# Expert blocks of a routed feed-forward: rows loaded from a register address and turned by VectorE instead of TensorE

## The chip, the cores and the metric

The kernel runs as one program on one core of one Trainium2 chip. Its time is device microseconds of one execution; five executions took 2359.26 to 2365.59 us, with a median of 2361.71 us. Engines are named as the profile names them: PE (TensorE matmul), PEld (its weight loads), DVE (VectorE), ACT (ScalarE), POOL (GpSimd), SP (SyncE, which here only issues transfers). SPq is SP's queue of transfer instructions.

## The reference

Eight images of 256 channels on 32 x 32 points pass through two layers, all in float32. The first is multi-head attention (8 heads, 64 channels each) with a residual. The second works on tokens (1024 per image, 256 channels): a softmax attention with one weight matrix, and then a mixture of experts, which is the part that the change touches.

```python
def _moe(tokens, router_w, w1, b1, w2, b2):          # E = 8 experts, D = F = 256
    logits = tokens @ router_w.T
    probs = jax.nn.softmax(logits, axis=-1)
    rw, re = jax.lax.top_k(probs, 2)
    rw = rw / jnp.maximum(rw.sum(-1, keepdims=True), 1e-12)
    combine = jnp.zeros((N, E)).at[jnp.arange(N)[:, None], re].set(rw)
    out = tokens
    for e in range(E):
        h = jax.nn.gelu(tokens @ w1[e] + b1[e], approximate=False)
        out = out + combine[:, e:e+1] * (h @ w2[e] + b2[e])
    return out
```

Each token takes part in two of eight experts, and a sum over its two experts' outputs, weighted by its gates, is added to it.

## The kernel before

**Stages.** The images 0 to 6 go one after the other through layer 0 and the token attention. At the end of each, `dispatch` scatters every token's 256 values twice into a DRAM table `rows`, once into the region of each of its two experts (7168 rows per expert). When image 7 has passed layer 0, `experts` (lines 1017 to 1106) computes the outputs of all scattered rows of images 0 to 6 into a DRAM table `y`. After that image 7's token attention runs, then its own experts (`dense`), while `Results` gathers the rows of `y` and adds them to images 0 to 6.

**Blocks.** `plan` cuts the experts' regions into 63 blocks of BR = 256 rows, and computes for each block where its rows start (`row_at`) and where its expert's weights stand (`w_at`). Both are only known on the chip. A block has these steps:

- `fetch` (L1020 to L1047): an indirect transfer on POOL's queue (L1026) brings the packed weights `wb`, 128 rows of 5128 bytes (out of bounds, so nothing moves, where the buffer already has the expert); there are four buffers. A second one (L1035) brings the 256 rows, two per partition, into `xr` (three buffers). Four PE transposes (L1044) turn them into the PSUM tile `px`, and a DVE copy (L1046) takes it to `xb`, where the 256 channels lie on partitions.
- `hidden` (L1049): four float32 products `ph` (L1054), which the profile counts as eight, and two Gelu activations on ACT (L1064) into `hT`.
- `collect` (L1072): four products `pe` (L1079), again eight in the profile, a DVE addition of the bias (L1088) into `yb`, and a store of `yb` to `y` from SP (L1093).

The loop issues `hidden(b-1)`, `fetch(b)`, `collect(b-2)`. A scheduler lays out each engine's list of instructions from this, and `tc.issue_after` makes it put one instruction behind another. Every engine runs its own list strictly in order. On PE a block reads `ph` of one block, `px` of the next one and `pe` of the block before.

**Queues.** SP holds, beside the y stores, the loads of images, the quarter moves `aT` of the token attention (L697), the loads of the sums `o` (L1153), of the dense weights (L1233, L1237) and the stores of the output (L1226). A transfer issued from SP or ACT takes one of eight completion semaphores in turn, and waits until the transfer that had it eight transfers before is complete.

**Packed weights.** `pack` (L283) copies w1, w2, b1 and b2 once, early in the program, into the DRAM table `wpack`, such that a row of it is what one partition of `wb` needs.

**Bookkeeping on DVE.** `places` (L991) computes for each image and choice, from the plan, which row of `y` a token's output will be; it is issued as one piece after block 4's addition. Its results are `kept` for the gathers.

Of the kernel before, what the change touches and what calls it, by code (L numbers as in the profile page):

```python
# [10 lines left out]
F32 = mybir.dt.float32  # L11
# [8 lines left out]
def kernel(  # L20
# [39 lines left out]
    NWB = 3  # L60
    NXB = NWB + 1

    dram = ctx.enter_context(tc.tile_pool(name="dram", bufs=1, space=bass.MemoryType.DRAM))
# [72 lines left out]
    for e in range(E):  # L136
# [14 lines left out]
    )  # L151
    r_iota = const.tile([P, 1], F32, name="r_iota")
    nc.gpsimd.iota(
        r_iota, [[1, 1]], base=0, channel_multiplier=R, allow_small_or_imprecise_dtypes=True
    )
    ones = const.tile([P, P], F32, name="ones")
# [52 lines left out]
    NB = NT // NH2  # L209
    SQ = 32  # L210
    NQ = P // SQ

# [68 lines left out]
    def pack():  # L281


        wp = wpack.rearrange("(e p) c -> e p c", p=P)
        for dc in range(NCC):
            nc.sync.dma_start(  # L286
                wp[:, :, ts(dc, FF)], w1.rearrange("e (dc p) f -> dc e p f", p=P)[dc]
            )
        at = NCC * FF
# [147 lines left out]
    def layer0(b, xT, begun, routing, xs):  # L437
# [138 lines left out]
        for at in range(last + LAG + 1):  # L576
# [28 lines left out]
            elif at == last + 1:  # L605
                divide(last)
            if at == 0:
# [318 lines left out]
    def plan(group):  # L926
# [41 lines left out]
        base = tmp("p_base", [E])  # L968
        nc.vector.tensor_scalar(base, first, -float(BR), r_iota, ALU.mult, ALU.add)
        work = tmp("p_work", [nb, E])  # L970
# [3 lines left out]
        nc.vector.scalar_tensor_tensor(lo, b_iota[:, :nb], float(BR), lo, ALU.mult, ALU.add)  # L974
        nc.vector.tensor_scalar_min(lo, lo, float(cap - R))
        nc.vector.scalar_tensor_tensor(lo, e_of, float(cap), lo, ALU.mult, ALU.add)
# [16 lines left out]
    def places(group):  # L993

        first = group.first
        for b in group.items:
            gate, kept = group.kept[b]
            ats = []
            for k, (row, exp) in enumerate(kept):
# [15 lines left out]
                ats.append(at)  # L1015
            group.kept[b] = gate, ats

    def experts(group):
        n = group.n
        row_at, w_at = group.where  # L1020

        wbs_x = [*wbs, one.tile([P, WROW], F32, tag="v", name="wb_x")]

        def fetch(b):
            wb = wbs_x[b % NXB]
            nc.gpsimd.indirect_dma_start(  # L1026
                out=wb[:, :],
                out_offset=None,
                in_=wpack[:, :],
                in_offset=bass.IndirectOffsetOnAxis(ap=w_at[:, b : b + 1], axis=0),  # L1030
                bounds_check=E * P - 1,
                oob_is_err=False,
            )
            xr = rowp.tile([P, R, D], F32, tag="xr", name=f"xr_{n}_{b}")
            nc.gpsimd.indirect_dma_start(  # L1035
                out=xr.rearrange("p r d -> p (r d)"),
                out_offset=None,
                in_=group.rows[:, :],
                in_offset=bass.IndirectOffsetOnAxis(ap=row_at[:, b : b + 1], axis=0),
            )  # L1040
            px = big(f"px_{n}_{b}")
            for dc in range(NCC):
                for r in range(R):
                    nc.tensor.transpose(px[:, ts(dc * R + r, P)], xr[:, r, ts(dc, P)], ident)  # L1044
            xb = two.tile([P, NCC, BR], F32, tag="xb", name=f"xb_{n}_{b}")
            nc.vector.tensor_copy(xb.rearrange("p c t -> p (c t)"), px[:, : NCC * BR])  # L1046
            return xb  # L1047

        def hidden(b, xb):  # L1049
            wb = wbs_x[b % NXB]  # L1050
            ph = big(f"ph_{n}_{b}")
            for fc in range(NFC):
                for dc in range(NCC):
                    nc.tensor.matmul(  # L1054
                        ph[:, ts(fc, BR)],
# [7 lines left out]
            for fc in range(NFC):  # L1063
# [6 lines left out]
                )  # L1070
            return hT

        def collect(b, hT):
            wb = wbs_x[b % NXB]
            py = acc(f"pe_{n}_{b}")
            at = NCC * FF
            for r in range(R):
                for fc in range(NFC):
                    nc.tensor.matmul(  # L1079
                        py[:, ts(r, D)],  # L1080
                        hT[:, fc, ts(r, P)],
                        wb[:, at + fc * D : at + (fc + 1) * D],
                        start=(fc == 0),
                        stop=(fc == NFC - 1),
                    )
            at += NFC * D + NFC
            yb = two.tile([P, R, D], F32, tag="yb", name=f"yb_{n}_{b}")
            added = nc.vector.tensor_add(  # L1088
                yb,
                py.rearrange("p (r d) -> p r d", d=D),  # L1090
                wb[:, at : at + D].unsqueeze(1).to_broadcast([P, R, D]),
            )
            nc.sync.dma_start(group.y[ts(b, BR), :].rearrange("(p r) d -> p r d", r=R), yb)  # L1093
            if b == NXB:
                with tc.issue_after(added.ins):
                    places(group)


        rows, hiddens = {}, {}
        for b in range(group.nb + 2):  # L1100
            if b - 1 in rows:
                hiddens[b - 1] = hidden(b - 1, rows.pop(b - 1))
            if b < group.nb:
                rows[b] = fetch(b)
            if b - 2 in hiddens:
                collect(b - 2, hiddens.pop(b - 2))

# [237 lines left out]
    for b in range(B):  # L1345
# [6 lines left out]
        if b + 1 < B:  # L1352
# [5 lines left out]
            continue  # L1358
        experts(groups[0])
        others = Results(groups[0])  # L1360
# [56 lines left out]
```

## Time and profile before

| What | Value |
|---|---|
| Median of five executions | 2361.71 us |
| The profiled execution's own time | 2360.97 us |
| Its span | 2359.0 us |
| Mean granted clock of PE | 0.992 |
| PE busy / DVE busy / ACT busy / POOL busy over the span | 98% / 64% / 46% / 18% |
| First PE transpose of `xr` starts / last product `pe` ends | 1859.8 us / 2128.8 us |
| POOL transfers of rows (L1035) | 63, 956 ns each on POOL |
| DVE copies of `px` (L1046) | 63, 691 ns each |
| SP's y stores (L1093) | 63, 320 ns each on SPq |

Times in the tables of groups are busy times of a whole group and the mean of one instruction; matmuls are pipelined, so that the mean of one (381 ns for `ph`) is longer than the distance between two. The distance is read from the chain of work that ended last, which gives a whole run of products its share of the time. The time of DMA packets is given as a share of the 16 DMA engines' time.

### The profile page before, as it was taken

How to read it: one execution, taken by the hardware profiler on the slowest of the kernel's cores; microseconds unless marked ns; L12 is line 12 of the kernel's file. 1: busy time of each engine (PE TensorE's matmuls, PEld its weight loads, DVE VectorE, ACT ScalarE, POOL GpSimd, SP SyncE). 2: the span in 40 equal slices, each digit the busy share in tenths (PEclk: the TensorE clock that was granted, in tenths of full speed). 3: DMA queues.
4: the chain of work that ended last, by engine and by line, in shares of the span. 5: the costliest groups of instructions: out<-in, count | busy, mean ns of one | idle time of the engine just before them, and what ended most of it. 6: DMA issues, size and time to landing. Idle time of an engine off the chain costs nothing.

```text
span 2359.0 us, 37255 instructions
## 1 busy us (share of the span) xinstructions
PE 2305.4 (98%) x13375; PEld 1256.3 (53%) x13375; DVE 1513.0 (64%) x3660; ACT 1092.3 (46%) x1954; POOL 421.4 (18%) x391
## 2 busy tenths in 40 slices
PE   9999999999999999999999999999999999999798
PEld 3345534653456345633563356335643588885465
DVE  5775577567855785578557855786578653334755
ACT  3663366346634663466346634563556422223311
POOL 0000012000200020002000300030003144544563
PEclk9999999999999999999999999999999999999899
DMA  8995201020102010201030102010201266665664
GB/s 296 385 386 140 63 17 39 13 51 15 41 9 54 10 46 6 57 8 48 3 61 6 50 1 45 21 35 1 45 19 61 88 213 221 206 201 143 156 176 110
DMA packets 219232, 209.23 MB, mean 89 GB/s; under 512 B 120200, under 2 KB 162856, under 8 KB 217256
## 3 DMA queue, kind: packets, MB, share of 16 engines
q1 hardware_dynamic: 192952, 139.13, 19.7%
q0 software_dynamic: 25008, 67.20, 9.3%
q8 instruction: 107, 1.75, 0.3%
q10 hardware_dynamic: 1088, 0.52, 0.1%
q14 instruction: 77, 0.63, 0.1%
HBM read 108.88 MB, written 110.90 MB: 93 GB/s over the span
## 4 chain that ended last, share of the span: by engine, by line
PE 81%; SPq 8%; DVE 5%; DMA 2%; issue 1%; ACT 1%; another core or an unknown queue 1%; POOL 0%; DVEq 0%; ACTq 0%; POOLq 0%
PE po L541 17%; PE psc L464 16%; PE py L713 8%; PE ps L672 7%; PE pqk L346 6%; SPq L270 5%; PE ph L1054 4%; PE pe L1079 4%; PE pr L638 4%; PE pv L383 4%; PE px L657 2%; PE pdy L1307 2%; PE pdh L1283 2%; PE pqk L324 2%; SPq L286 1%
## 5 line engine op out<-in xcount | busy, mean ns | idle before, releaser
L505 ACT ACTIVATE ex<-psc,nmax 128x1024 f32<-128x1024 f32 x512 | 570.5, 1115 | 304.2 <-DVE scrap L488 217.7
L464 PE MATMUL psc<-qk,qk 64*64 64x512 f32 x4096 | 575.7, 593 | 7.8 <-ACT ex L505 7.7
L541 PE MATMUL po<-ex,vs 64*64 64x512 f32 x4096 | 569.6, 592 | 1.4 <-DVE vs L521 0.5
L488 DVE TENSOR_SCALAR_CACHE_REDUCE scrap<-psc,nmax 128x512 f32<-128x512 f32 x512 | 384.5, 751 | 160.7 <-PE psc L464 133.2
L479 DVE TENSOR_REDUCE nmax<-psc 128x1 f32<-128x512 f32 x512 | 350.8, 685 | 9.5 <-PE psc L464 9.5
L464 PEld LDWEIGHTS psc<-qk,qk 64*64 64x64 f32 x4096 | 178.9, 132 | 285.6 <-ACT ex L505 136.8
L541 PEld LDWEIGHTS po<-ex,vs 64*64 64x64 f32 x4096 | 174.1, 132 | 275.7 <-issue 84.7
L713 PE MATMUL py<-n,aT 128*128 128x256 f32 x1024 | 237.3, 386 | 7.5 <-DVE aT L706 4.0
L713 PEld LDWEIGHTS py<-n,aT 128*128 128x128 f32 x1024 | 197.9, 194 | 59.7 <-issue 26.9
L672 PE MATMUL ps<-nT,xa 128*128 128x512 f32 x512 | 228.6, 592 | 0.0
L917 POOL DMA_INDIRECT rows<-n,d_at x112 | 109.2, 975 | 660.8 <-DVE nmax L479 658.0
L844 POOL TENSOR_TENSOR t<-t,n 128x2048 f32<-128x2048 f32 x8 | 36.3, 4533 | 880.0 <-DVE n L238 880.0
L697 ACT COPY aT<-sq 32x256 f32<-32x256 f32 x384 | 154.4, 402 | 82.0 <-DVE sq L690 50.5
L346 PE MATMUL pqk<-xT,wqkv 128*128 128x512 f32 x384 | 171.2, 599 | 0.0
L672 PEld LDWEIGHTS ps<-nT,xa 128*128 128x128 f32 x512 | 96.6, 190 | 102.4 <-issue 94.7
L680 DVE TENSOR_REDUCE nmax<-ps 128x1 f32<-128x1024 f32 x64 | 77.9, 1217 | 84.8 <-PE ps L672 80.4
L311 ACT ACTIVATE qk<-pqk,b_qks 128x512 f32<-128x512 f32 x124 | 85.6, 691 | 95.7 <-PE pqk L346 77.0
L1163 POOL DMA_INDIRECT yk<-y,yat x112 | 111.3, 993 | 90.3 <-issue 29.6
L346 PEld LDWEIGHTS pqk<-xT,wqkv 128*128 128x128 f32 x384 | 71.0, 190 | 99.9 <-issue 76.8
L383 PE MATMUL pv<-wqkv,xT 128*128 128x512 f32 x256 | 121.7, 603 | 1.1 <-DVE v L391 1.0
L638 PE MATMUL pr<-wo,res 128*128 128x256 f32 x512 | 111.9, 379 | 0.3 <-ACT res L560 0.3
L1064 ACT ACTIVATE hb<-ph,wb 128x256 f32<-128x256 f32 x96 | 40.3, 471 | 144.2 <-issue 82.5
(191 smaller groups left out, 2443.8 us busy)
## 6 DMA issues: line engine op xcount, KB each, us to landing
rows<-wb SPq DMA_DIRECT2D x7, 8192.0 KB
y<-yb SPq DMA_DIRECT2D x63, 256.0 KB
aT<-sq SPq DMA_DIRECT2D x384, 32.0 KB
xs<-in_x_dram SPq DMA_DIRECT2D x64, 128.0 KB
out_dram<-oT SPq DMA_DIRECT2D x60, 128.0 KB
xT<-in_x_dram SPq DMA_DIRECT2D x7, 1024.0 KB
sums<-t SPq DMA_DIRECT2D x7, 1024.0 KB
o<-sums SPq DMA_DIRECT2D x7, 1024.0 KB
```

What stands on the lines that cost most here:

```text
L270: nc.sync.dma_start(group.rows.rearrange("(p c r) d -> p c (r d)", p=P, r=2)[:, c : c + 32], zero.unsqueeze(1).to_broadcast([P, 32, 2 * D]),)
L346: mm = nc.tensor.matmul(pq[:, ts(n, 512)], wqkv[:, cc, t, ts(g, P)], xT[:, cc, ts(n, 512)], start=(cc == 0), stop=(cc == NCC - 1),)
L383: nc.tensor.matmul(pv, self.xT[:, cc, ts(i, P)], wqkv[:, cc, 2, :], start=(cc == 0), stop=(cc == NCC - 1),)
L464: mm = nc.tensor.matmul(pss[at, h][ts(c, DK), ts(n, 512)], k[r, j * P + c * DK : j * P + (c + 1) * DK], q[r, ts(n, 512)], start=True, stop ...
L479: firsts[at, h] = nc.vector.tensor_reduce(nmax, pss[at, h][:, ts(0, 512)], AX.X, ALU.max, negate=True)
L488: seconds[h] = nc.vector.tensor_scalar(scrap, pss[at, h][:, ts(1, 512)], -1.0, nmaxes[at, h], ALU.mult, ALU.min, accum_out=nmax,)
L505: nc.scalar.activation(ex, pss.pop((at, h)), AF.Exp, bias=nmaxes.pop((at, h)), scale=1.0, accum_out=sums[at][:, h : h + 1],)
L541: mm = nc.tensor.matmul(po[n][ts(h, DK), :], vss[at][keys, h, :], exps[at, h][keys, ts(n, 512)], start=(j == 0 and turn == 0), stop=(j == ...
L638: nc.tensor.matmul(pr[:, :C], res[:, g, ts(i, P)], wo[:, g, :], start=(g == 0), stop=(g == NPAIR - 1))
L672: nc.tensor.matmul(psc[:, ts(n, 512)], xa[:, ec, ts(i, P)], nT[:, ec, ts(n, 512)], start=(ec == 0), stop=(ec == NCC - 1),)
L697: move(to[ts(k, SQ), a], since[ts(a, SQ), k])
L713: nc.tensor.matmul(py[:, :D], aT[m], n1[:, m, :], start=(m == 0), stop=(m == NT - 1))
```

## The change

The rows of a block are no longer gathered by POOL. SP reads the block's first row number into a register (`value_load`) and issues four direct transfers from that address, one for each quarter of 64 channels, into 32 partitions each: every row falls into four pieces of 64 float32 (256 bytes), 1024 pieces a block. One DVE instruction (`nc.vector.transpose`, squares of 32 x 32) then turns `xr` into `xb`, and PE's four transposes and the DVE copy from PSUM are gone. Partition 32k + c of `xb` now has the channels 64k + c and 64k + 32 + c, so `pack` writes w1 in that order, in eight transfers rather than two.

The loop has one more stage: `hidden(b-2)`, `fetch(b)`, `turned(b-1)`, `collect(b-3)`. `issue_after` puts the squares behind the last division of layer 0, `collect`'s products behind the latest `hidden`'s last product, and each block's addition behind the squares of a block two further on. The y store is issued from ACT; it writes row r·128 + p from partition p, in pieces of 1024 bytes (before: 2p + r, two adjoining rows, 2048 bytes). `places` becomes a generator, of which one piece is taken after each block's addition from block 4 on. The plan's row numbers are those of a block's first row, the same on all partitions.

```diff
+    SQ = 32
+    NQ = P // SQ
+    DQ = D // NQ
+    RUN = BR // SQ
@@ pack
-        for dc in range(NCC):
-            nc.sync.dma_start(
-                wp[:, :, ts(dc, FF)], w1.rearrange("e (dc p) f -> dc e p f", p=P)[dc]
-            )
+        src = w1.rearrange("e (k cc c) f -> k cc e c f", k=NQ, c=SQ)
+        for k in range(NQ):
+            for cc in range(NCC):
+                nc.sync.dma_start(wp[:, ts(k, SQ), ts(cc, FF)], src[k, cc])
@@ layer0
-                divide(last)
+                evicted["divided"] = divide(last)
@@ plan
-        nc.vector.tensor_scalar(base, first, -float(BR), r_iota, ALU.mult, ALU.add)
+        nc.vector.tensor_scalar_mul(base, first, -float(BR))
-        nc.vector.tensor_scalar_min(lo, lo, float(cap - R))
+        nc.vector.tensor_scalar_min(lo, lo, float(cap - BR))
@@ places
-            group.kept[b] = gate, ats
+                if k > 0:
+                    group.kept[b] = gate, ats
+                yield
@@ experts, fetch
-            xr = rowp.tile([P, R, D], F32, tag="xr", name=f"xr_{n}_{b}")
-            nc.gpsimd.indirect_dma_start(
-                out=xr.rearrange("p r d -> p (r d)"),
-                out_offset=None,
-                in_=group.rows[:, :],
-                in_offset=bass.IndirectOffsetOnAxis(ap=row_at[:, b : b + 1], axis=0),
-            )
-            px = big(f"px_{n}_{b}")
-            for dc in range(NCC):
-                for r in range(R):
-                    nc.tensor.transpose(px[:, ts(dc * R + r, P)], xr[:, r, ts(dc, P)], ident)
+            xr = rowp.tile([P, RUN, DQ], F32, tag="xr", name=f"xr_{n}_{b}")
+            with tc.issue_after(loads[-1].ins) if loads else nullcontext():
+                at = nc.sync.value_load(
+                    row_at[0:1, b : b + 1], min_val=0, max_val=E * group.cap - BR
+                )
+            mine = group.rows[bass.ds(at, BR), :].rearrange("(s t) (k d) -> k t s d", s=RUN, k=NQ)
+            for k in range(NQ):
+                loads.append(nc.sync.dma_start(xr[ts(k, SQ)], mine[k]))
+            return xr
+
+        def turned(b, xr):
             xb = two.tile([P, NCC, BR], F32, tag="xb", name=f"xb_{n}_{b}")
-            nc.vector.tensor_copy(xb.rearrange("p c t -> p (c t)"), px[:, : NCC * BR])
-            return xb
+            with tc.issue_after(behind.ins):
+                squares = nc.vector.transpose(
+                    xb.rearrange("p cc (s t) -> p s cc t", t=SQ),
+                    xr.rearrange("p s (cc c) -> p s cc c", c=SQ),
+                )
+            return xb, squares
@@ experts, collect
+            with tc.issue_after(last.ins):
 ...
+            with tc.issue_after(squares.ins):
 ...
-            nc.sync.dma_start(group.y[ts(b, BR), :].rearrange("(p r) d -> p r d", r=R), yb)
-            if b == NXB:
+            nc.scalar.dma_start(group.y[ts(b, BR), :].rearrange("(r p) d -> p r d", r=R), yb)
+            if b >= NXB:
                 with tc.issue_after(added.ins):
-                    places(group)
+                    next(placed, None)
@@ experts, loop
-        for b in range(group.nb + 2):
-            if b - 1 in rows:
-                hiddens[b - 1] = hidden(b - 1, rows.pop(b - 1))
+        for b in range(group.nb + 3):
+            if b - 2 in rows:
+                hiddens[b - 2], last = hidden(b - 2, rows.pop(b - 2))
             if b < group.nb:
                 rows[b] = fetch(b)
-            if b - 2 in hiddens:
-                collect(b - 2, hiddens.pop(b - 2))
+            if b - 1 in rows:
+                rows[b - 1], squares = turned(b - 1, rows.pop(b - 1))
+            if b - 3 in hiddens:
+                collect(b - 3, hiddens.pop(b - 3), last, squares)
```

More of the change, by code (lines that the diff above doesn't have):

```diff
@@ L151 @@
     )
-    r_iota = const.tile([P, 1], F32, name="r_iota")
-    nc.gpsimd.iota(
-        r_iota, [[1, 1]], base=0, channel_multiplier=R, allow_small_or_imprecise_dtypes=True
-    )
     ones = const.tile([P, P], F32, name="ones")
@@ L209 @@
     NB = NT // NH2
-    SQ = 32
-    NQ = P // SQ
     def bcast(t, n):
@@ L1015, in places, with experts @@
                 ats.append(at)
-            group.kept[b] = gate, ats
-    def experts(group):
+                if k > 0:
+                    group.kept[b] = gate, ats
+                yield
+    def experts(group, behind):
         n = group.n
         row_at, w_at = group.where
+        loads = []
         wbs_x = [*wbs, one.tile([P, WROW], F32, tag="v", name="wb_x")]
@@ L1033, in fetch @@
             )
-            xr = rowp.tile([P, R, D], F32, tag="xr", name=f"xr_{n}_{b}")
-            nc.gpsimd.indirect_dma_start(
-                out=xr.rearrange("p r d -> p (r d)"),
-                out_offset=None,
-                in_=group.rows[:, :],
-                in_offset=bass.IndirectOffsetOnAxis(ap=row_at[:, b : b + 1], axis=0),
-            )
-            px = big(f"px_{n}_{b}")
-            for dc in range(NCC):
-                for r in range(R):
-                    nc.tensor.transpose(px[:, ts(dc * R + r, P)], xr[:, r, ts(dc, P)], ident)
-            xb = two.tile([P, NCC, BR], F32, tag="xb", name=f"xb_{n}_{b}")
-            nc.vector.tensor_copy(xb.rearrange("p c t -> p (c t)"), px[:, : NCC * BR])
-            return xb
+            xr = rowp.tile([P, RUN, DQ], F32, tag="xr", name=f"xr_{n}_{b}")
[8 more added lines that the diff above has]
+        def turned(b, xr):
+            xb = two.tile([P, NCC, BR], F32, tag="xb", name=f"xb_{n}_{b}")
+            with tc.issue_after(behind.ins):
[4 more added lines that the diff above has]
+            return xb, squares
         def hidden(b, xb):
@@ L1053, in hidden @@
                 for dc in range(NCC):
-                    nc.tensor.matmul(
+                    last = nc.tensor.matmul(
                         ph[:, ts(fc, BR)],
@@ L1070, in hidden, with collect @@
                 )
-            return hT
-        def collect(b, hT):
+            return hT, last
+        def collect(b, hT, last, squares):
             wb = wbs_x[b % NXB]
@@ L1076, in collect @@
             at = NCC * FF
[L1077 to L1085, printed above, removed]
+            with tc.issue_after(last.ins):
+                for r in range(R):
+                    for fc in range(NFC):
+                        nc.tensor.matmul(
+                            py[:, ts(r, D)],
+                            hT[:, fc, ts(r, P)],
+                            wb[:, at + fc * D : at + (fc + 1) * D],
+                            start=(fc == 0),
+                            stop=(fc == NFC - 1),
+                        )
@@ L1086, in collect @@
             at += NFC * D + NFC
             yb = two.tile([P, R, D], F32, tag="yb", name=f"yb_{n}_{b}")
[L1088 to L1093, printed above, removed]
-            if b == NXB:
+            with tc.issue_after(squares.ins):
+                added = nc.vector.tensor_add(
+                    yb,
+                    py.rearrange("p (r d) -> p r d", d=D),
+                    wb[:, at : at + D].unsqueeze(1).to_broadcast([P, R, D]),
+                )
@@ L1095, in collect @@
+            nc.scalar.dma_start(group.y[ts(b, BR), :].rearrange("(r p) d -> p r d", r=R), yb)
+            if b >= NXB:
                 with tc.issue_after(added.ins):
-                    places(group)
+                    next(placed, None)
         rows, hiddens = {}, {}
-        for b in range(group.nb + 2):
-            if b - 1 in rows:
-                hiddens[b - 1] = hidden(b - 1, rows.pop(b - 1))
+        placed = places(group)
+        assert group.nb - NXB >= 2 * len(group.items)
+        last = squares = None
@@ L1358 @@
             continue
-        experts(groups[0])
+        experts(groups[0], evicted["divided"])
         others = Results(groups[0])
```

## The prediction

> **What bounds the kernel now.** I read first the busy shares, then the busy times by stage around the experts. PE is busy for 98% of the span, so only what shortens PE's list, or makes it wait, can move the time.
>
> ```profile
> PE 2305.4 (98%) x13375; PEld 1256.3 (53%) x13375; DVE 1513.0 (64%) x3660; ACT 1092.3 (46%) x1954; POOL 421.4 (18%) x391
> 1881.00:2125.00 244.00, 241.28 (x1228) 209.47 (x1228) 96.80 (x200) 51.76 (x124) 115.41 (x118) 1.00 0.66 216
> ```
>
> The second line is the expert stage: of 244.0 us PE is busy 241.3, DVE 96.8, ACT 51.8, at a granted clock of 1.00, with the DMA engines 66% busy. PE is the bound here too; it stands still for 2.7 us. The chain of waits inside the stage shows what a block is made of:
>
> ```profile
> 1922.53 1.73 PE pe L1079 x8
> 1924.26 1.73 PE ph L1054 x8
> 1925.99 0.44 PE px L1044 x4
> 1926.43 1.73 PE pe L1079 x8
> ```
>
> A block is 1.73 + 1.73 + 0.44 = 3.90 us of PE, and nothing else is on the chain. The first and the 61st y store are issued at 1885.66 and 2124.34 us (timeline of SP), 3.98 us apart on average; that is the period T I count with, of which 0.08 are the few stalls.
>
> The groups of instructions by line give the operations that change hands, the DMA view what the transfers cost:
>
> ```profile
> L1044 PE MATMUL px<-ident,xr 128*128 128x128 f32 x252 | 38.1, 273 | 0.0
> L1046 DVE COPY xb<-px 128x512 f32<-128x512 f32 x63 | 43.5, 691 | 90.4 <-PE px L1044 65.1 <-PE ph L1054 25.3
> L690 DVE STREAM_TRANSPOSE sq<-ex 128x1024 f32<-128x1024 f32 x48 | 59.7, 1243 | 62.8 <-ACT ex L683 54.9 <-DMA aT<-sq 6.3 <-issue 1.6
> L1035 POOL DMA_INDIRECT xr<-rows,row_at x63 | 60.2, 956 | 43.2 <-PE px L1044 23.2 <-issue 15.6 <-DMA rows<-n,d_at 2.4
> ```
>
> ```profile
> q0 software_dynamic: 5606, 14.46, 47.3%
> q1 hardware_dynamic: 3634, 6.62, 17.4%
> ...
> q1 hardware_dynamic: 7110, 0.86, 28.5%
> ...
> q1 hardware_dynamic: 2716, 1.11, 89.9%
> ...
> q1 hardware_dynamic: 818, 0.83, 54.9%
> ```
>
> These are queues (packets, MB, share of 16 engines) in four windows: 1950 to 2050 us (two lines: POOL's queue; SP's with 25 y stores), 220 to 240 us (`aT` moves, 128-byte pieces), 1693 to 1700 us (`xs` loads, 2047 pieces of 512 bytes beside 669 small ones), 195 to 200 us (`wpack`, 1024-byte pieces). Share times window times 16 engines over packets is the price of a piece: y's 2048 bytes 85 ns, 128 bytes 12.8 ns, 512 bytes 45 ns (the small ones taken off), 1024 bytes 54 ns. The packet records add 256-byte pieces, 17.7 ns each (`b_v`, DRAM to SBUF, at 9 to 12 us), and xr's present packets of 4096 bytes, 213 ns in the expert stage against about 159 where the DMA engines are quiet.
>
> ```profile
> L423 SPq DMA_DIRECT2D xs<-in_x_dram x64: 311/449/1414, 7.5 to 1697.0; - x64
> L697 SPq DMA_DIRECT2D aT<-sq x384: 120/609/1538, 212.2 to 2199.6; - x192
> L1093 SPq DMA_DIRECT2D y<-yb x63: 319/320/344, 1885.7 to 2131.5; - x63
> ```
>
> What an issue costs SP (min/median/max ns): 320 for the plain y store, 449 for `xs`, which has the shape of the new loads (32 partitions, 8 pieces each, from DRAM), 609 for `aT`. Some 45 ns lie between two.
>
> **The change part by part.**
>
> PE's transposes: 63 x 0.44 us = 27.7 us off the path that sets the end. This is certain as long as PE stays the bound; T would be 3.46 us, with today's stalls 3.54.
>
> DVE: a copy of 691 ns goes, squares of 128x512 come. L690 and L430 take 1243 and 1219 ns for twice as many elements, so I take 620. DVE is busy 40% of the stage, so the difference costs nothing. What changes is the order: the squares of block b+2 stand ahead of block b's addition. If rows come late, the addition waits behind the squares, with it the y store, the weight buffer, and next PE, whose `ph` of b+2 needs the squares.
>
> POOL loses 63 x 956 ns and the waits on `px`; nobody needed it earlier, nothing is gained but a prompter weight transfer.
>
> ACT gets 63 y stores. Its four output stores stand in the trace at 375 to 465 ns each; with Gelu's 2 x 0.42 us ACT is busy 1.3 of 3.5 us a block. Queued behind the store is the next block's Gelu, which its `pe` needs only after another 3.46 us: cover enough, cost zero.
>
> SP: a y store goes, four loads come: 4 x (0.449 + 0.045) = 1.98 us, plus register arithmetic and the register's load. No row shows these. Bounds: below 5 x 17 ns (SPq's event instructions) with nothing for the load; above, the load as slow as a whole transfer is from issue to first packet (y: 1.0 us median) and 0.1 us for each of five arithmetic steps. SP is then 2.1 to 3.5 us a block, and with `aT`'s 609 ns up to 4.1. I take 3.1, below 3.46: hidden by PE. The Trainium skill ("DMA: Bandwidth & Descriptors", Latency and other measured facts) gives a floor of about 600 ns for such a register load; no run here shows it. By it alone SP would be near 2.7 us and hidden too.
>
> DMA engines: today 0.66 x 3.98 = 2.63 us of all 16 engines a block. Off go xr (64 x 213 ns / 16 = 0.85) and y (128 x 85 / 16 = 0.68). y in 256 pieces of 1024 bytes: between half of 85 and 54 ns, I take 48: 0.77. xr in 1024 pieces of 256 bytes: below the 12.8 ns of a 128-byte piece (0.82 us), above the 45 ns of a 512-byte piece (2.88 us). The nearest row is `b_v`, same size and direction, 17.7 ns; loaded as the stage is I scale it by 213/159 to 23.7 ns: 1.52 us. Sum 2.63 - 0.85 - 0.68 + 0.77 + 1.52 = 3.39 us a block, 96% of a 3.54 us period; with the bounds 2.69 to 4.75. The same page (Specifications) asks for at least 512 bytes a piece for line rate, with slower read-modify-write below: a rule against this change. The rows bear it out only in part: 17.7 ns for 256 bytes is 14 GB/s an engine, 85 ns for 2048 is 24. At line rate xr would cost 0.68 us, by the row 1.52.
>
> The new wait: of the eight completion semaphores a block uses five, so the loads of block b+5 wait, in the built order, for y store b. From the end of block b's `pe`: about 0.95 us to the y issue (0.2 semaphore, 0.69 addition), y complete (1.6 to 4.6 us from issue to the last packet in the packet records, median 2.7), three more load issues 1.5, landing of the last load (taken as y's median, 2.7), squares 0.62: 8.5 us, against three blocks, 10.4 us. It holds on average, but not when weights come: they move in about half the blocks, in runs of about four, 128 x 265 ns / 16 = 2.1 us each, and the DMA demand of such a block is 3.39 - 1.0 + 2.1 = 4.5 us, over the period by 1.0. Four such blocks gather 4 us, of which the weights' lead of three blocks hides more than half; I charge 1.6 us per eight blocks, 0.2 us a block, 63 x 0.2 = 12.6 us. Bounds: 0, and the whole DMA excess of the rival below.
>
> Start of the stage: `ph` of block 0 moves in front of layer 0's last products, with a Gelu table load (1.28 us) and a Gelu between the two ACT copies of `res` (588 ns). The squares can't start before the division ends at 1860.6 us, so PE waits for them; then three quarters of `ph` (1.3), the rest of the products (1.5), and ACT's copy, table load, Gelu, copy (2.9) put L638 at about 1867.5 instead of 1863.72, of which 2.2 us is work done early. With 0.8 us of today's idle before the second `ph` gone, I charge 1 us (0 to 3.8).
>
> `pack`'s eight transfers rather than two move the same packets at a time when SPq waits for room behind the fill of `rows`; `places`' pieces move 14 x 1.0 us of DVE that has time; both zero. Later, three 1 MB loads of `o` instead of two fall at the end of the experts, beside gathers: zero, bounded by 1 MB's 3 us.
>
> Sum: -27.7 + 12.6 + 1 = -14 us. The profiled execution took 2360.97 us (span 2359.0 and 2.0 around it), 0.7 below the median; 2361 - 14 = 2347 us.
>
> **The rivals.**
>
> 1. *PE keeps everything* (no new wait): T 3.54, -27.7 + 1 = -27: 2334 us. For it: the bounds of DMA reach down to 2.69. Against: 96% of DMA time by the nearest row.
> 2. *DMA becomes the bound, slower.* Place: the row pieces. If a piece costs p ns the demand is 1.87 + 0.064 p us. It passes today's T (less the 1 us at the start) at 3.96 us, p = 33 ns. At the 45 ns of `xs`, also 32-partition loads of short pieces, T = 4.75, 63 x 0.77 + 1 = +49: 2410 us. For it: `xs` fills its DMA engines. Against: its pieces are twice as long and 4 KB apart.
> 3. *SP becomes the bound.* With `aT`'s issue time four loads are 2.6 us; if the register's load with its arithmetic is over 1.35 us, T passes 3.96. At 1.5 us T = 4.1: +9, 2370 us. For it: nothing else in the kernel loads a register, so nothing limits its price. Against: `xs` has the very shape and takes 449.
> 4. *Nothing in the sum:* waits of 0.4 us a block eat the gain: 2357 to 2366.
>
> **How the numbers follow.** Partial gain, 2338 to 2356 us: 0.36, the likeliest, hence 2347. Full gain, below 2338: 0.17. Rival 4: 0.09. DMA: 0.22, SP: 0.16. Faster 0.53, same 0.09, slower 0.38, where 0.2% (4.7 us) is about what a measurement of this kernel can tell from no change. The range 2334 to 2395 leaves out about half of rival 2 and little at the bottom; the forecast's own is 2338 to 2356.
>
> **What would show it.** L1044 and the DVE copies are gone; PE busy in the stage 28 us less. A block's chain shows 1.73 + 1.73 with now and then a wait of PE `ph` for the squares, and of these for DMA xr, mostly while weights move. The DMA share of the stage is above 0.85, a 256-byte packet about 24 ns. On SPq a register load below 1 us. I am wrong if the squares wait for xr in every block (then packets above 33 ns, or SPq never idle), or if PE never waits.

## The result and the profile after

The change moves the time by nothing that can be measured: 2362.89 us (median of 27 executions, 2356.71 to 2372.41) against 2363.8 us before on the same chip (50 executions), a ratio of 0.9999 with a 95% interval of 0.9993 to 1.0005. The forecast was 2347 us. The profiled execution took 2364.1 us, with a span of 2361.3 us.

The busy shares of the changed kernel, from the page, and the expert stage from the table by windows (columns: window, its length, busy us of PE, PEld, DVE, ACT and POOL with their instructions, granted clock, DMA share, GB/s):

```profile
PE 2285.6 (97%) x13123; PEld 1232.3 (52%) x13123; DVE 1513.6 (64%) x3660; ACT 1092.8 (46%) x1955; POOL 358.8 (15%) x327
```

```profile
1881.00:2125.00 244.00, 223.80 (x1008) 190.74 (x1007) 101.00 (x211) 53.45 (x126) 58.87 (x59) 0.99 0.76 214
```

The transposes are gone, and PE has not been given other work: in the same 244 us it was busy for 241.28 before and is busy for 223.80 now. It stands still for 20 us of this window, where it stood still for 2.7. From the first block's bias addition to the last one's, 62 blocks later, DVE's timeline has 245.9 us before and 242.9 now: 3.97 and 3.92 us a block. Of the 62 distances 32 are below 3.6 us, and the undisturbed ones are 3.455 us; over that floor the others lose 28.7 us together. Before, the blocks lost 4 us in this way (245.9 less 62 x 3.90).

The chain of work that ended last shows what PE waits for. This is its part from 1921 to 1948 us (start, us, what):

```profile
1921.87 1.74 PE pe L1085 x8
1923.63 0.69 DVE yb L1095
1924.36 2.58 DMA y<-yb
1927.05 0.32 SPq L1042
...
1929.25 4.15 DMA xr<-rows
...
1934.16 0.65 DVE yb L1095
1934.85 5.94 DMA y<-yb
1940.90 0.32 SPq L1042
...
1944.67 2.98 DMA xr<-rows
1947.66 0.72 DVE xb L1048
...
1948.43 1.99 PE ph L1059 x8
```

The chain that was nothing but PE before now goes through transfers: a store of `y` (2.58 us), the issues of SP that come right behind its end, rows (4.15 us), a bias addition, a store again (5.94 us, weights are moving), SP, rows, squares, and at last `ph`. The chain does not follow one block (the addition at 1934.16 belongs to another block than the rows before it, which it follows on DVE), but every kind of link in it belongs to a loop that the kernel before did not have.

The waits between 1885 and 2130 us (engine and line, waited for what: us in all, times, longest):

```profile
DVE xb L1048 <- DMA xr<-rows: 68.6, 33, 4.9
SPq L1042 <- DMA y<-yb: 48.6, 43, 5.2
PE ph L1059 <- DVE xb L1048: 18.8, 15, 3.0
```

The squares wait for rows 33 times. SP waits 43 times before it issues row loads, for the end of a `y` store. PE waits for the squares.

How long the moved operations take, from the views of single lines (count, min/median/max in ns, first and last start):

```profile
L1048 DVE STREAM_TRANSPOSE xb<-xr x63: 669/712/714, 1863.8 to 2118.5; 128x512 f32<-128x512 f32 x63
L1037 SPq TENSOR_LOAD <-row_at x63: 199/277/804, 1807.8 to 2113.0; - x63
L1037 SPq FUSED_REGOPS  x63: 152/152/194, 1808.4 to 2113.4; - x63
L1042 SPq DMA_DIRECT2D xr<-rows x252: 208/321/1507, 1840.7 to 2116.0; - x126
L1100 ACTq DMA_DIRECT2D y<-yb x63: 366/366/436, 1888.2 to 2131.1; - x63
```

And the queues between 1950 and 2050 us (packets, MB, share of 16 engines):

```profile
q1 hardware_dynamic: 27598, 6.65, 29.9%
q0 software_dynamic: 3600, 7.88, 24.8%
q10 hardware_dynamic: 6971, 6.73, 20.9%
```

SP's queue (q1) carries the row pieces, POOL's (q0) the weights alone, ACT's (q10) the `y` stores. The packet records of the stage (1895 to 2130 us) give 18.5 ns for a row piece of 256 bytes, 50.2 ns for a piece of 1024 bytes of `y` and 252 ns for a weight row.

One thing stands ahead of the blocks, and the prediction had not seen it. PE's timeline at the end of image 7's layer 0 (start, us, engine, line, what; in brackets the idle time before it and what ended that):

```profile
1841.78 1.09 PE L539 MATMUL po<-ex,vs 64*64 64x512 f32 x8 [2.06 <-SPq L549]
...
1864.56 1.53 PE L1059 MATMUL ph<-xb,wb 128*128 128x256 f32 x6 [1.47 <-issue]
...
1870.30 14.08 PE L636 MATMUL pr<-wo,res 128*128 128x256 f32 x64
```

L549 is an empty instruction on SP. In layer 0 PE's products for one half of its array are put behind those of the other half by such relays, `relay = nc.sync` for all images but the first. SP issues the first twelve row loads from 1840.71 to 1849.36 us, with their register loads, and the relays stand among them in its list. Ahead of the first of these loads SP waits for the last scatter into `rows`, which the view of SP's waits from 1830 to 1850 us shows as `SPq L1042 <- DMA rows<-n,d_at: 3.5, 1, 3.5`; the relays behind it pass at 1841.12 and 1841.71 us, though the products that they wait for had ended by 1839.74, and PE loses 2.06 us. (At 1808.81 us PE stands 4.26 us behind another relay, which stands behind SP's first register load and its 12.9 us of waiting for `row_at`. That costs only 0.6 us, since the kernel before stands 4.39 us there for ACT.) Then `ph` of block 0 stands in PE's list before layer 0's last products and waits 1.47 us. Counted from a product that all kernels have in common (at 1781.75 us before, 1782.22 after), block 0's addition ends 2.1 us later than before, although three groups of transposes (1.3 us) are no longer ahead of it.

### The profile page after: what moved, and what is told of

The parts are those of the page before. It is cut to its first block, busy times and chain, and to the rows that moved or that the text cites. A ratio compares the mean times of both kernels' runs of the same rounds, so it can differ in the third digit from the quotient of the medians.

```text
span 2361.3 us, 37654 instructions
## 1 busy us (share of the span) xinstructions
PE 2285.6 (97%) x13123; PEld 1232.3 (52%) x13123; DVE 1513.6 (64%) x3660; ACT 1092.8 (46%) x1955; POOL 358.8 (15%) x327
## 4 chain that ended last, share of the span: by engine, by line
PE 80%; DMA 5%; DVE 5%; issue 4%; POOL 3%; SPq 1%; ACT 1%; another core or an unknown queue 1%; DVEq 0%; POOLq 0%; ACTq 0%
PE po L539 19%; PE psc L462 18%; PE ps L670 8%; PE py L711 8%; PE pqk L344 7%; PE pr L636 5%; PE pv L381 4%; PE px L655 2%; PE ph L1059 2%; DMA xr<-rows 2%; PE pe L1085 2%; POOL yk L1175 2%; PE pqk L322 2%; DMA y<-yb 2%; DVE n L236 1%
## 5 line engine op out<-in xcount | busy, mean ns | idle before, releaser
L1059 PE MATMUL ph<-xb,wb 128*128 128x256 f32 x384 | 93.4, 386 | 17.9 <-DVE xb L1048 16.4
```

## The experiments

The theory read from this profile, called L: the row loads of block b+5 wait for the store of `y` of block b, because both take the same eight completion semaphores, and the way from store to store is about as long as the five blocks that it may take. The medians of its links, from the timelines and the packet records of blocks 11 to 62:

| Link | us |
|---|---|
| end of `pe` to the issue of the store of `y` | 0.75 |
| issue to the store's last packet | 2.74 |
| last packet to SP's first load of block b+5 | 0.68 |
| first to fourth load | 1.62 |
| fourth issue to the last packet of rows | 2.59 |
| last packet to the start of the squares | 0.99 |
| squares | 0.71 |
| sum | 10.1 |

From the end of `pe` of block b to `ph` of block b+5 PE has three blocks of work, 10.4 us. The loop fits with 0.3 us to spare. Where weights move, the store's median is 3.35 and the rows' 3.30 us, which adds 1.3 us; elsewhere they are 2.15 and 1.83 us.

The rivals: B, three buffers of `xr` are too few; D, the DMA engines can't deliver rows, `y` and weights any faster, in whatever order; and, from the second group of runs on, W, the weights come too late by themselves.

**First group: where the wait sits.** On this chip the kernel before took 2372.4 us (25 executions), and the changed one was not run on it; the three timed runs are read against each other and by their traces.

`y` stored from POOL:

```diff
-            nc.scalar.dma_start(group.y[ts(b, BR), :].rearrange("(r p) d -> p r d", r=R), yb)
+            nc.gpsimd.dma_start(group.y[ts(b, BR), :].rearrange("(r p) d -> p r d", r=R), yb)
```

> The changed kernel with one edit: the y stores are issued from POOL instead of ACT, so they take no completion semaphore of the eight that the row loads share. Theory L (the loop): in the changed kernel the loads of block b+5 begin 0.45 to 0.8 us after y store b is complete, in nearly every block; store 2.7, next issue 0.6, four issues 1.6, landing 2.6, start of the squares 1.05, squares 0.71, then four groups of products and the addition, 8.0, make 17.3 us for five blocks, as much as five blocks of products (5 x 3.46); any delay by a weight transfer is added to the time. Without the wait the period falls from 3.92 to 3.46-3.55 us and the time by 20 to 28 us: 2335 to 2343 us. Theory D (the DMA engines cannot deliver more): demand is 3.06 us of 16 engines a block plus queueing, the waits of PE for rows stay where weights move, 2355 to 2365 us. Theory B (three xr buffers are too few): nothing changes, 2360 to 2366 us.

Measured: 2367.18 us, 0.9977 of the kernel before (0.9965 to 0.9989). The gain that L expected is not there, but the waits are not those of D either. The waits of this kernel from 1885 to 2130 us:

```profile
DVE xb L1048 <- DMA xr<-rows: 1.4, 2, 1.0
...
PE ph L1059 <- DMA wb<-wpack,w_at: 6.4, 7, 2.5
PE ph L1059 <- DMA wb_x<-wpack,w_at: 5.9, 4, 2.1
```

The wait for rows went from 68.6 to 1.4 us, as L expects. The edit does one thing more: the packets of `y` have 4096 bytes there instead of 1024, so that the run with the loosened loop below is the cleaner test. In place of the rows PE waits for weights. Their transfers now stand behind the stores of `y` on POOL, as this kernel's chain shows (start, us, what):

```profile
1995.07 8.25 DMA wb<-wpack,w_at
2003.45 1.97 PE ph L1059 x8
```

So the edit removed one wait and made another. Its time says nothing about L, its waits do: counted from a common product, its last addition ends 4.2 us earlier than in the changed kernel, but from there to the end it takes 239.4 us instead of 230.2, which was not followed up.

Four buffers of `xr`:

```diff
-    rowp = ctx.enter_context(tc.tile_pool(name="rowp", bufs=3))
+    rowp = ctx.enter_context(tc.tile_pool(name="rowp", bufs=4))
```

> The changed kernel with four buffers of xr instead of three. Theory L: the loads wait for the y stores, not for a buffer: no change, within 2 us of 2363. Theory B: the loads start a block earlier, period 3.5 us, 2338 to 2348 us. Theory D: no change.

Measured: 2364.89 us, 0.9975 (0.9963 to 0.9986) on that chip. The mean distance of two blocks is 3.92 us, as in the changed kernel, and the squares wait as long for rows. B is out.

No weights after the first four blocks:

```diff
+        nc.vector.tensor_scalar_add(hi[:, NXB:], hi[:, NXB:], float(E * P))
         w_at = keep.tile([P, NBMAX], I32, tag="w_at", name=f"w_at_{n}", bufs=2)
```

> The changed kernel, which leaves out all weight transfers after the first four blocks (their addresses are out of bounds, so the transfers are issued and move nothing; later blocks use the wrong expert's weights). Theory L: with no weights moving the store takes 2.15 instead of 2.7 us and the landing 1.83 instead of 2.6, the loop is 16.0 us against 17.3 of products: waits of PE for rows disappear, period 3.46-3.5, 2334 to 2340 us, although the DMA engines still move all rows and stores and each load still waits for its store. Theory D says the same of the time, with a DMA share falling to about 0.6. If the loop is too long even without weights, the period stays above 3.6 us, 2346 us or more.

Measured (this kernel leaves out the weights of the later blocks), in a single execution: 2338.61 us, 3.49 us a block. Its windows:

```profile
1950.00:2000.00 50.00, 50.00 (x234) 43.91 (x233) 19.88 (x30) 12.26 (x30) 14.30 (x15) 1.00 0.59 155
```

PE is busy without a break, though every load still waits for its store. The order alone costs nothing; it takes the weights, with which the store and the rows last longer (medians of 2.14 and 1.98 us here), to make the loop longer than PE's work. D expects the same of this run; the next group separates the two.

The start of the stage:

```diff
+            evicted["turned"] = turned[1]
...
-            with tc.issue_after(loads[-1].ins) if loads else nullcontext():
+            with tc.issue_after(loads[-1].ins if loads else evicted["turned"].ins):
...
+                    with tc.issue_after(evicted["mixed"].ins):
                         last = nc.tensor.matmul(
```

(`evicted["mixed"]` is the last product `pr`.)

> The changed kernel with the first row loads put behind the last of SP's relay instructions of layer 0 (they pass PE's turn from one half of the array to the other), and the first products ph put behind the products pr. In the changed kernel PE stands still for 2.06 us at 1841.8 us waiting for that relay (L549) while SP is busy with the first twelve loads, and 1.47 us at 1864.6 for the first squares; the pr products stand 6.67 us later than before the change, of which 2.2 us are ph moved forward. Theory S (SP's early loads hold up the relay, early ph holds up PE): the first y store comes 2.5 to 3.5 us earlier and the time falls by as much: 2359 to 2361 us against 2363. Rival: the blocks' loop gives back what the start gains, since its rows are then the later ones: 2362 to 2364 us.

Measured: 2367.34 us, 0.9975 (0.9966 to 0.9985), no better than the run with four `xr` buffers beside it. The start does what was expected: this kernel's PE timeline has `pr` at 1863.21 us with 0.68 us of idle time ahead of it (1870.30 in the changed kernel), and the first addition ends 3.7 us earlier. But the last addition ends 3.0 us later than in the changed kernel: the blocks' mean distance is 4.03 us. The rival of this expectation was right. Why the blocks then lose more than they had won was not followed up.

**Second group: the loop loosened in its place.** To move the wait without moving a transfer to another queue, the loads run ahead where semaphores are given out, and the store of `y` is put behind them in that order (an edge for the scheduler alone, no wait on the chip). PE, ACT and POOL keep their lists.

The changed kernel again, on the chip of this group:

> The changed kernel as it is, on the same chip as the next three, for comparison: within 0.4% of the kernel before.

Measured: 2362.84 us, 1.0000 of the kernel before (0.9988 to 1.0012; before 2362.13 us).

The loads of block b+6 wait for store b:

```diff
+LATER = mybir.DependencyInfo(mybir.DependencyClass.NoSync, mybir.DependencyReason.DATA)
...
-    rowp = ctx.enter_context(tc.tile_pool(name="rowp", bufs=3))
+    rowp = ctx.enter_context(tc.tile_pool(name="rowp", bufs=4))
...
+            with tc.issue_after(stores[b - 2].ins) if b - 2 in stores else nullcontext():
                 for fc in range(NFC):
                     nc.scalar.activation(
...
-            nc.scalar.dma_start(group.y[ts(b, BR), :].rearrange("(r p) d -> p r d", r=R), yb)
+            stored = nc.scalar.dma_start(
+                group.y[ts(b, BR), :].rearrange("(r p) d -> p r d", r=R), yb
+            )
+            tc.add_manual_dep(stored.ins, loads[-1].ins.name, LATER)
+            stores[b] = stored
...
+            if b + 1 < group.nb:
+                rows[b + 1] = load(b + 1)
             if b < group.nb:
-                rows[b] = fetch(b)
+                fetch(b)
```

(`fetch` keeps the weights, `load` has the register load and the four transfers.)

> The changed kernel with the y store of block b put behind the loads of block b+4 (before: b+3) where semaphores are given out, and four xr buffers: the loads of block b+6 now wait for store b, not those of b+5. Order on PE, ACT and POOL is the same. Theory L: the loop of 17.3 us (more where weights move) now has six blocks, 20.7 us, so the waits of the squares for rows fall from 69 us to under 25 and the time by 12 to 20 us against the changed kernel. Theory W: the rows come in time, but where weights move PE then waits for these instead (their transfer can only be issued after the addition four blocks before, about 6 us ahead of the products that need them, and took 3 to 8 us with POOL's stores): waits of PE for wb of 10 to 25 us appear, and the time falls by 3 to 12 us. Theory D (the DMA engines deliver no more): rows as late as now, within 3 us.

Measured: 2349.51 us, 0.9936 (0.9916 to 0.9955), 13.3 us less than the changed kernel on the same chip. The waits from 1885 to 2130 us:

```profile
DVE xb L1051 <- DMA xr<-rows: 3.7, 5, 1.2
...
PE ph L1062 <- DMA wb<-wpack,w_at: 5.2, 6, 1.8
```

The same order of work on PE, the same transfers, one block more between a store and the loads that wait for it (of a block's four loads it is now the third that waits, before it was the first): the wait for rows falls from 68.6 to 3.7 us. The fourth buffer of rows had changed nothing by itself. That is L shown in its place, and D is out as the cause in the changed kernel. The same view also puts 21.5 us ahead of the additions down to rows (`DVE yb L1099 <- DMA xr<-rows: 21.5, 11, 3.2`), but all additions from block 2 on, save the last two, begin within 0.3 us of the end of their products or of DVE's instruction before. What is left is W: PE's list has twelve gaps of 0.16 to 1.8 us ahead of `ph`, 10.2 us together. `ph` waits for nothing but its squares and its weights; in front of all but one of the gaps the squares had ended 1.4 us or more before, and in front of all twelve a weight transfer had landed 0.7 to 1.1 us before. Mean distance 3.74 us.

One block more (five `xr` buffers, and `ph` of block b put behind `pe` of block b-2, which keeps PE's list):

> As the run before, one block further: the loads of block b+7 wait for store b, five xr buffers. Theory L: the waits for rows are gone, period 3.46 to 3.55 us, 20 to 28 us less than the changed kernel. Theory W: no better than with one block, since PE waits for the weights. Theory D: within 3 us of the changed kernel.

Measured: 2351.57 us, 0.9960 (0.9945 to 0.9974). No better than one block, as W had it.

The same with the start of the stage as above:

> As the run before, and in addition the first row loads behind the last of SP's relay instructions of layer 0 and the first products ph behind pr. With the loop loosened what the start loses is no longer made up later: 3 to 4 us less than the run before, by theory L 24 to 31 us less than the changed kernel, by W 6 to 16.

Measured: 2352.48 us, 0.9956 (0.9939 to 0.9972): no difference to the run before. In the profiled executions the first addition is 4.2 us earlier and the end 3.0 us; the medians don't bear this out.

**Third group: earlier weights, and one part undone.** Before took 2359.31 us here.

A fifth buffer of weights beside the loosened loop:

```diff
-    NXB = NWB + 1
+    NXB = NWB + 2
...
-        wbs_x = [*wbs, one.tile([P, WROW], F32, tag="v", name="wb_x")]
+        wbs_x = [
+            *wbs,
+            one.tile([P, WROW], F32, tag="v", name="wb_x"),
+            one.tile([P, WROW], F32, tag="xa", name="wb_y"),
+        ]
```

> As the run where loads wait for the store six blocks before (2349.5 us), with a fifth buffer of weights (in a tile that stands free during the experts), so that a weight transfer is issued a block, 3.5 us, earlier; five instead of four transfers for an expert. In that run PE stood still 10 us in twelve gaps of 0.16 to 1.8 us ahead of ph, and in front of each the weights had landed 0.7 to 1.1 us before (theory W). Theory W: these gaps go, the mean period falls from 3.74 to 3.5-3.6 us, 6 to 12 us less. Theory D (the DMA engines are full where weights move): a fifth transfer only adds 2 us of DMA time for each expert, rows and weights come as late as before or later, within 3 us, or slower.

Measured: 2341.34 us, 0.9922 (0.9905 to 0.9938); by itself this can't be told from the 0.9936 (0.9916 to 0.9955) without the fifth buffer on another chip. Its profiled execution took 2351.1 us, some 10 more than the three others (2339.46 to 2341.45), so its trace is read for the kind of the waits alone: PE's gaps are no longer behind a landing of weights but 0.06 us behind the end of squares, and

```profile
DVE xb L1055 <- DMA xr<-rows: 42.7, 23, 3.5
```

the squares wait for rows again. A fifth transfer for each expert makes the DMA engines busier (share 0.93 between 1890 and 2090 us, 0.77 in the changed kernel, 0.82 with the loosened loop), and rows and stores take longer: from issue to last packet 3.18 and 3.99 us in the median, against 2.59 and 3.48 with four buffers. The loop of six blocks is at its end as that of five was.

With the start of the stage in addition:

> As the run before, with the first row loads behind SP's last relay instruction of layer 0 and the first ph behind pr: the first addition of the experts comes 3.5 to 4 us earlier (as measured with that edit alone). If nothing behind it gives this back: 3 to 4 us less than the run before. If the loops give it back, as with that edit alone, no difference.

Measured: 2343.9 us, 0.9937 (0.9920 to 0.9953): no gain, within the uncertainty of the run before.

The fifth buffer alone, a single execution:

> The changed kernel with the fifth buffer of weights alone; the loads wait for the store five blocks before as in the changed kernel. If the rows are the first limit (theory L), earlier weights give nothing: mean period 3.85 to 4.0 us, 2358 to 2368 us, the squares still wait 60 us or more for rows. If weights alone had been the limit, a period of 3.7 or less and 2350 us or less.

Measured: 2370.34 us, 4.09 us a block; the squares wait 83.3 us for rows. Earlier weights help nothing while the loop through the store is the limit; their added transfers lengthen it.

The store of `y` back on SP:

> One part undone: the y store is issued from SP again, not from ACT; the row loads from a register and DVE's squares stay. SP holds the store in its list between loads, and the store waits for the addition, so loads that stand behind it wait for that addition too, not only for a semaphore. If ACT as the place of the store is worth nothing (the prediction costs it at zero): within 3 us of the changed kernel. If the loads behind the store are held up by it: the waits for rows grow, period 4.1 to 4.4 us, 10 to 30 us slower.

```diff
-            nc.scalar.dma_start(group.y[ts(b, BR), :].rearrange("(r p) d -> p r d", r=R), yb)
+            nc.sync.dma_start(group.y[ts(b, BR), :].rearrange("(r p) d -> p r d", r=R), yb)
```

Measured: 2374.4 us, 1.0066 (1.0049 to 1.0083). The waits of this kernel:

```profile
DVE xb L1048 <- DMA xr<-rows: 108.4, 51, 4.5
```

```profile
SPq L1100 <- DVE yb L1095: 35.8, 35, 2.3
SPq L1100 <- DVE p_hot L1005: 18.5, 12, 2.9
```

SP stands at the store until the addition is done, and the loads behind it stand with it; the squares wait 108.4 instead of 68.6 us for rows. The size was missed: the distance of two blocks is 3.97 us in the profiled execution, not 4.1 to 4.4. That execution took 2368.7 us, 5.7 below the median, so the trace carries only a part of the 15 us.

**Fourth group: both loosened.** Before took 2359.3 us here. Loads of block b+7 wait for store b, five buffers of weights:

> As the run with the store six blocks before and five buffers of weights (2341.3 us), and the loads wait for the store seven blocks before, with five xr buffers. In that run the last 10 us of gaps stand right behind the squares again (0.06 us), which wait 43 us for rows. If that is still the loop through the store: the waits for rows fall under 10 us, the period to 3.5-3.6 us, 4 to 8 us less. If it is the DMA engines (theory D: where weights move, rows, stores and weights together need more than the engines give, whatever the order): rows still late, period 3.65-3.72, within 3 us.

Measured: 2338.53 us, 0.9913 (0.9896 to 0.9929), 3.55 us a block. The waits of DVE:

```profile
DVE yb L1104 <- DMA y<-yb: 37.7, 15, 5.0
DVE xb L1055 <- DMA xr<-rows: 9.1, 7, 2.2
```

The wait for rows fell to 9.1 us as expected; between 1890 and 2090 us PE is busy for

```profile
1890.00:2090.00 200.00, 196.42 (x903) 170.62 (x902) 89.13 (x186) 47.34 (x114) 56.21 (x57) 1.00 0.95 260
```

196.4 of 200 us, against 182.5 in the changed kernel, with the DMA engines 95% busy. Against the run with the same loop and four buffers of weights (0.9960, 0.9945 to 0.9974) the fifth buffer is a gain clear of both intervals, which is W shown; against the loop of six blocks with five buffers (0.9922, 0.9905 to 0.9938) the ratio can't be told apart.

With the start of the stage:

> As the run before, with the first row loads behind SP's last relay instruction of layer 0 and the first ph behind pr: the first addition 3.5 to 5 us earlier. If the stage no longer gives it back, 3 to 5 us less than the run before; else the same.

Measured: 2333.34 us, 0.9891 (0.9875 to 0.9908), 5.2 us below the run before on the same chip. That this is the start's gain isn't shown. Counted from a common product, the first addition ends 4.0 us earlier than in the run before, but the last one only 0.4 us earlier: the mean distance is 3.61 us instead of 3.55, and between 1890 and 2090 us PE is busy for less than there:

```profile
1890.00:2090.00 200.00, 195.20 (x892) 168.00 (x892) 86.71 (x182) 46.61 (x112) 55.23 (x56) 1.00 0.95 260
```

The other 4.3 us are won behind the experts. From the last addition to the end the profiled kernels of this document take 222.5 (this one) to 239.4 us, and what makes this differ was not followed up. The version is 1.1% below the kernel before, and its time is close to that of the prediction's first rival (2334 us).

Three buffers of `yb` in it:

```diff
-            yb = two.tile([P, R, D], F32, tag="yb", name=f"yb_{n}_{b}")
+            yb = two.tile([P, R, D], F32, tag="yb", name=f"yb_{n}_{b}", bufs=3)
```

> As the fastest run so far (2333.3 us, 0.9891 of the kernel before), with three instead of two buffers of yb. There the additions wait 51 us for earlier y stores, in 19 places, the longest 4.8 us, and PE then stands still ahead of pe or ph for 0.2 to 1.0 us; the DMA engines are 95% busy between 1890 and 2090 us. If the last waits are a matter of buffers: they go, 2 to 6 us less, 2327 to 2331 us (0.986 to 0.989). If the DMA engines are the limit by now: the same waits appear at the rows or the weights, 2331 to 2336 us (0.988 to 0.991).

Measured on another chip: 2343.25 us where before takes 2371.04, 0.9878 (0.9862 to 0.9895). The additions' wait for stores is gone, and another has come:

```profile
DVE xb L1056 <- DMA xr<-rows: 28.6, 21, 4.5
DVE yb L1105 <- DMA y<-yb: 5.0, 2, 3.0
```

```profile
1890.00:2090.00 200.00, 191.79 (x871) 163.49 (x870) 85.84 (x178) 45.34 (x109) 54.70 (x55) 1.00 0.93 255
```

The ratio can't be told from the 0.9891 of the run without the buffer, PE is busy no longer than there (191.8 against 195.2 us), and the waits only moved from the stores to the rows. This speaks for D at this point: with the DMA engines 93 to 95% busy a wait that is removed comes back at another transfer. That a kernel with fewer packets would lose the rest was not tried.

## Why the prediction was wrong

**PE's transposes: right.** 252 transposes are gone, and the undisturbed distance of two blocks fell from 3.90 to 3.455 us, just the 0.44 us that were counted.

**DVE's squares: 712 ns, not 620.** With DVE 41% busy in the stage this would cost nothing by itself; it is one of the links of the loop.

**POOL: right**, nothing was gained there. **ACT: nearly right in its price** (366 ns, forecast 375 to 465). What the prediction didn't ask is what the place is worth: back on SP the store costs 0.66%.

**SP: right that it is hidden, and too dear.** A row load's issue takes 321 ns and the register load 277 ns, with 152 ns of arithmetic: with the arithmetic and the moves between, two blocks' first loads stand no closer than 2.7 us where nothing is waited for (2.74 for blocks 18 and 19), against a forecast of 3.1. The floor of about 600 ns that the Trainium skill gives for such a register load ("DMA: Bandwidth & Descriptors", Latency and other measured facts) is not what this trace shows; its shortest is 199 ns. The rival in which SP is the bound is out.

**DMA engines: right in kind, somewhat too dear.** 18.5 ns for a row piece (forecast 23.7), 50.2 for a piece of `y` (48). What failed is the scaling by 213/159: `b_v`'s 17.7 ns hardly grew, and 159 ns is also the median of the old row packets in the stage, whose mean is 215. The share of 0.76 (the prediction's sign was one above 0.85) at 3.92 us a block is 2.98 us a block, not 3.39. The rival in which the row pieces make the DMA engines the bound from 33 ns on is out: at 18.5 ns they don't. The rule of the same page (Specifications) that asks for 512 bytes and more is borne out in part: 256 bytes in 18.5 ns are 13.8 GB/s an engine, 1024 in 50.2 ns are 20.4.

**The new wait: the step that failed.** The prediction found the wait, its place and its cause, and the runs confirm them. The term that was mis-sized is its sum of 8.5 us against 10.4. It took the store's and the rows' times well (2.74 and 2.59 us, both taken as 2.7), but let each link begin at the end of the one before. The trace has 0.68 us between a store's last packet and SP's next load, and 0.99 us between the rows' last packet and the squares. With them the sum is 10.1 us: there was no slack of 1.9 us to take up the weights, only 0.3. So the charge of 0.2 us a block on top of 0.08 of old stalls became 0.46 us. From the first addition to the last the forecast is 245.9 less 60 transposes of 0.44 plus 12.6, 232.1 us; the trace has 242.9. These 10.9 us are most of the miss.

**Start of the stage: 1 us was charged, 3.4 measured** (2.1 later in spite of 1.3 us of transposes less; the bounds were 0 to 3.8). The prediction counted the `ph` moved forward, and not that SP is also the relay of PE's halves: its list was looked at for transfers, and the relays are no transfers. Nor did it see that a load in that list waits, and the relay with it. With the start moved the first addition came 3.7 to 5.4 us earlier in the four pairs of runs above; how much of it reaches the end is open.

**The end of the stage** was put at zero. In the profiled execution the attention of image 7 begins 1.2 us after the last addition's end instead of 0.5 before it, and takes 1.0 us longer from there: 2.7 us in all. No run was made for this, and it lies well within the 222.5 to 239.4 us that this part takes in the runs above.

10.9, 2.4 and 2.7 us, with 0.5 lost before the stage and 0.8 outside the span, make 17.3; from the forecast 2347 to the profiled 2364.1 it is 17.1.

**The rivals.** The fourth, waits of 0.4 us a block that eat the gain, 2357 to 2366 us, is what happened, at 0.46 us; it had been given 0.09. A time like the first's 2334 us was reached (2333.34), but with more than the change: the loads two blocks further from the stores, two more buffers of rows, one more of weights, and the start moved. That the number agrees is in part chance, since a block takes 3.61 us there, not the rival's 3.54.

## What to carry to other kernels

When a loop of waits is summed from a trace, add what lies between its links (here 0.7 us from a transfer's last packet to the next issue, 1.0 us to the next engine's instruction), and compare it with the time that it may take where other traffic is heaviest, not on average. Completion semaphores that are given out in turn tie unrelated transfers to each other: look up which transfer a load really waits for, and move that by the order in which they are given out; more buffers alone did nothing here. A queue that gets new work may do something else for another engine that isn't a transfer, and that stands still behind a load that waits; read its whole list.

## What the runs showed of the hardware that was not expected

- A row piece of 256 bytes takes 18.5 ns in a stage where the DMA engines are 76% busy, hardly more than the 17.7 ns of the same size early in the kernel. The packets of 4096 bytes that it replaced took 215 ns in the mean and 159 in the median in that stage.
- A register load on SP takes 277 ns in the median, 199 to 804.
- An SP that waits at a load holds up PE: an empty relay instruction behind a load that waited 3.5 us for a scatter cost PE 2.06 us.
